# Per-strip DRAM tensors for a GNN layer's rows and partial sums, loaded from ScalarE's queue

## The chip, the cores and the metric

The kernel runs on one core of a Trainium2 chip. A core has five engines that run their own instruction streams: TensorE (PE, matrix products and transposes), VectorE (DVE), ScalarE (ACT), GpSimd (POOL) and SyncE (SP, which here only starts DMA transfers). ACT and POOL can start transfers too. An engine takes its instructions in the order of its stream and waits on semaphores; a transfer raises a semaphore when it has landed.

The metric is the device time of one execution in microseconds (us), the median over several runs. Lower is better.

## The reference: two graph layers on 3327 rows

Rows `x` (3327 x 128, padded to 3328) and a sparse symmetric adjacency `adj` (about 2% of the entries are not zero) go through two layers with a residual each. Layer 0 is a GATv2 attention with four heads, layer 1 a graph convolution:

```
h = relu(layernorm(x));  x = x + gatv2(h, adj, w1, w2, a, Wlin, w)      # layer 0
h = relu(layernorm(x))                                                   # layer 1
A_t = adj + I;  D_inv = rowsum(A_t) ** -0.5
x = x + relu(D_inv[:, None] * (A_t @ (D_inv[:, None] * (h @ W.T + b))))
```

Layer 1 is a dense product of the adjacency with 128-wide rows, so it can only be finished for a block of rows when layer 0 is finished for every block.

## The kernel before: blocks, strips and what each queue issues

**Blocks.** The 3328 rows are 26 blocks of 128 (`NB = 26`). Layer 0 runs block by block: POOL gathers the neighbours' rows (L595), PE transposes them (L622), VectorE makes the scores' input (L638), PE forms scores (L657) and sums (L670, L690). The generator `close` ends a block: ACT normalises (L754), PE and ACT apply two products (L771, L774, L782), VectorE writes the block's new rows `xn` (L786), SP stores them in DRAM (L788), ACT centres them (L793, L794), PE transposes (L798) and multiplies by layer 1's weights (L806), VectorE adds the bias (L809) and ACT puts the result into `x_sb` (L811). From then on the block is a column of layer 1's product.

**Strips.** Layer 1 is computed for strips of four blocks (`NS = 7`; strip 6 has two). A strip is one sum in PSUM, 128 x 512, over 26 columns, each column one matrix product of `x_sb[:, j]` with a 128 x 512 piece of the transposed adjacency (L1006). The pieces wait in DRAM (`AT_d`) and are brought in by L916, 11 columns at a time, alternately from SP and POOL. Much of the sum is made before the end, while layer 0 still runs: `part1` (columns known when the strip's own blocks are prepared, L379 to L387) and, for strips 1 to 3, `part2` (twelve more columns, L922 to L948). Both are stored in DRAM, `part1_d` and `part2_d`, and so are the new rows, `xn_d`. The last phase, `layer1`, multiplies the columns that are left: 26 for strip 0, then 12, 8, 4, 12, 8 and 4.

**The last phase in detail.** Strips 0 and 1 (`front`) are multiplied while block 25 is being closed; the column of block 25 itself comes last for both. `strip_in(s)` starts the loads of the strip's rows (L961), its `part1` (L963) and its `part2` (L965), each 256 KB; it is called at the fifth column of a strip, or at the last one where there are fewer or where the strip is in front. `strip_out(s)` ends a strip, three columns after its last one: VectorE adds `part2` (L973) and `part1` (L975), PE transposes the sum (L982), VectorE adds the block's own row and scales (L983, L984), takes the relu and adds the residual (L985), and ACT stores the result (L986). Strip 0 has no partial sums; ACT copies its sum (L977).

**Order.** The instructions of this phase stand in the order in which the Python code emits them (`tc.manual_schedule`); the framework adds the semaphore waits. SP issues, in this order: the pieces L916, strip 0's rows, more pieces, strip 1's three loads, block 25's store L788, the last three pieces, and then the loads of strips 2 to 6. ACT's stream in this phase is block 25's activations and the seven stores L986. Every transfer of SP and of ACT is given one of eight semaphores in turn (called lanes below), and its issue waits until the transfer before it on the same lane has landed. Buffers: `r0` (rows, and the sum in its second half) has three, `r1` (`part1`) two.

Of the kernel before, what the change touches and what calls it, by code (L numbers as in the profile page):

```python
# [9 lines left out]
F32 = mybir.dt.float32  # L10
# [5 lines left out]
P = 128  # L16
# [3 lines left out]
BANK = 512  # L20
# [211 lines left out]
def _sparse_layers(tc, nc, x, adj, w1, w2, a, wlin, w, gw, gb, gb_sb, gwT, x_sb, dinv, flag, ident, out):  # L232
# [13 lines left out]
    NP, D = x.shape  # L246
# [10 lines left out]
    with ExitStack() as l0:  # L257
        res = l0.enter_context(tc.tile_pool(name="res", bufs=1))
        dram = l0.enter_context(tc.tile_pool(name="dram", bufs=1, space=bass.MemoryType.DRAM))
        tables = [dram.tile([(NP + 1) * ROW], F32, name=f"table{k}") for k in range(2)]  # L260
        hT_d = dram.tile([P, NP], F32, name="hT_d")
        xn_d = dram.tile([NP, D], F32, name="xn_d")
        part1_d = dram.tile([D, NP], F32, name="part1_d")
        part2_d = dram.tile([D, NP], F32, name="part2_d")
        NS = -(-NB // 4)
        TURN = NP * P + HALF
        AT_d = dram.tile([NB * TURN], F32, name="AT_d")
        w1_sb = res.tile([P, H, D], F32, name="w1_sb")
# [59 lines left out]
        def bank():  # L328
            return ps_tr.tile([P, 4, P], F32, name="tr").rearrange("p a b -> p (a b)")
# [23 lines left out]
        def prep(b, k):  # L353
# [21 lines left out]
            def known_step(j0, js, at):  # L375
                assert all(blks[j0 + q].closed for q in js)
                pq = bank()
                for q in js:
                    nc.tensor.matmul(pq[:, :P], x_sb[:, j0 + q, :], at[:, q, :], start=(q == 0), stop=(q == js[-1]))  # L379
                yield  # L380
                if j0 == 0:
                    k.part1 = pb.tile([P, P], F32, name="part1", bufs=1)
                    nc.scalar.copy(k.part1, pq[:, :P])
                else:
                    nc.vector.tensor_add(k.part1, k.part1, pq[:, :P])
                if j0 + len(js) == finished(b):
                    nc.sync.dma_start(part1_d[:, b * P:(b + 1) * P], k.part1)  # L387

            known = []

# [353 lines left out]
        def close(k, hb):  # L744
            ag, b = k.ag, k.b
            yield

            rec = pv.tile([P, 2], F32, name="rec")
            nc.vector.reciprocal(rec, ag[:, :, WORK - 1])
            yield  # L750
            yield
            agn = pv.tile([P, 2, D], F32, name="agn")
            for u in range(2):
                nc.scalar.activation(agn[:, u, :], ag[:, u, :D], AF.Copy, scale=rec[:, u:u + 1])  # L754
            yield
            yield
            yield
            pt = ps_tr.tile([P, 4, P], F32, name="tr")
            for u in range(2):
                nc.tensor.transpose(pt[:, u, :], agn[:, u, :], ident)  # L760
            if hb == 0:
                k.agT = pv.tile([P, 16, H, 8], F32, name="agT")
            nc.scalar.copy(k.agT[:, 8 * hb:8 * hb + 8].rearrange("p t h q -> p (t h q)"), pt[:, :2].rearrange("p a b -> p (a b)"))
            yield
            if hb == 0:
                return

            yield
            po = ps_tr.tile([P, 4, P], F32, name="tr")
            for h in range(H):  # L770
                nc.tensor.matmul(po[:, h, :].rearrange("p (t q) -> p t q", q=8), wlinT[:, h, :], k.agT[:, :, h, :],  # L771
                                 start=True, stop=True)
            outT = pv.tile([P, H, P], F32, name="outT")
            nc.scalar.copy(outT, po)  # L774
            yield
            nc.vector.scalar_tensor_tensor(outT, outT, SLOPE, outT, op0=OP.mult, op1=OP.max)
            yield
            yield
            yield
            py = ps_tr.tile([P, 4, P], F32, name="tr")  # L780
            for h in range(H):
                nc.tensor.matmul(py[:, 0, :], outT[:, h, :], w_sb[:, h, :], start=(h == 0), stop=(h == H - 1))  # L782
            yield
            xn = pv.tile([P, D], F32, name="xn")
            st = pb.tile([P, 1], F32, name="st")
            nc.vector.scalar_tensor_tensor(xn, x_sb[:, b, :], 1.0, py[:, 0, :], op0=OP.mult, op1=OP.add, accum_out=st)  # L786
            nc.vector.tensor_scalar(st, st, -1.0 / D, None, op0=OP.mult)
            nc.sync.dma_start(xn_d[b * P:(b + 1) * P, :], xn)  # L788
            yield

            two = pv.tile([P, 2, D], F32, name="agn")
            cen, sq = two[:, 0], two[:, 1]
            nc.scalar.activation(cen, xn, AF.Relu, bias=st, scale=1.0)  # L793
            nc.scalar.activation(sq, xn, AF.Square, bias=st, scale=1.0, accum_out=k.dv[:, :1])  # L794
            yield
            yield
            pt = ps_tr.tile([P, 4, P], F32, name="tr")
            nc.tensor.transpose(pt[:, 0, :], cen, ident)  # L798
            nc.scalar.copy(sq, pt[:, 0, :])
            nc.vector.tensor_scalar(k.dv[:, :1], k.dv[:, :1], 1.0 / D, EPS, op0=OP.mult, op1=OP.add)  # L800
            yield
            rs = pb.tile([P, 2], F32, name="rs")
            yield from inv_root(rs, k.dv[:, :2])
            nc.vector.tensor_mul(dinv[:, b:b + 1], rs[:, 1:], k.dv[:, 2:])
            ph1 = ps_tr.tile([P, 4, P], F32, name="tr")
            nc.tensor.matmul(ph1[:, 0, :], sq, gwT, start=True, stop=True)  # L806
            yield
            yield
            nc.vector.scalar_tensor_tensor(cen, ph1[:, 0, :], rs[:, :1], gb_sb, op0=OP.mult, op1=OP.add)  # L809
            yield  # L810
            nc.scalar.activation(x_sb[:, b, :], cen, AF.Copy, scale=dinv[:, b:b + 1])  # L811
            k.closed = True
            yield
# [3 lines left out]
        for b in range(NB):  # L817
            k = Blk()
# [101 lines left out]
        def begin():  # L920

            work = [(s, j) for s in early for j in early[s]]  # L922
            pairs = [work[i:i + PAIR] for i in range(0, len(work), PAIR)]
            if not work:
                return
            thirds = pa.tile([P, NP], F32, name="adjb")[:, :3 * PAIR * BANK].rearrange("p (k j i) -> p k j i", k=3, j=PAIR)

            def bring(k):
                if k < len(pairs):
                    for to, of in columns(thirds[:, k % 3], pairs[k]):  # L930
                        nc.sync.dma_start(to, of)

            for k in range(3):
                bring(k)
            for _ in range(14):
                yield
            po = None
            for i, (s, j) in enumerate(work):
                assert blks[j].closed
                if j == early[s][0]:  # L940
                    po = bank()
                nc.tensor.matmul(po, x_sb[:, j, :], thirds[:, i // PAIR % 3, i % PAIR], start=(j == early[s][0]), stop=(j == early[s][-1]))  # L942
                if i % PAIR == PAIR - 1:
                    bring(i // PAIR + 3)
                if j == early[s][-1]:
                    part2 = pv.tile([P, H, P], F32, name="outT").rearrange("p h i -> p (h i)")
                    nc.scalar.copy(part2, po)
                    nc.sync.dma_start(part2_d[:, 4 * s * P:4 * s * P + BANK], part2)  # L948
                for _ in range(4):
                    yield  # L950

# [3 lines left out]
        def strip_in(s):  # L955

            n = min(4, NB - 4 * s)
            r0 = pr.tile([P, 2, BANK], F32, name="r0", bufs=3).rearrange("p k (b d) -> p k b d", b=4)[:, :, :n]
            r1 = pr.tile([P, 2, BANK], F32, name="r1").rearrange("p k (b d) -> p k b d", b=4)[:, :, :n]
            rows = slice(4 * s * P, (4 * s + n) * P)  # L960
            nc.sync.dma_start(r0[:, 0], xn_d[rows, :].rearrange("(b p) d -> p b d", p=P))  # L961
            if finished(4 * s):
                nc.sync.dma_start(r1[:, 0], part1_d[:, rows].rearrange("p (b i) -> p b i", b=n))  # L963
            if s in early:
                nc.sync.dma_start(r0[:, 1], part2_d[:, rows].rearrange("p (b i) -> p b i", b=n))  # L965
            return n, rows, r0, r1

        def strip_out(s, po, n, rows, r0, r1):
# [19 lines left out]

        front = range(min(2, NS - 1))
        work = [(s, j) for s in front for j in range(first_column(s), NB - 1)]  # L990
        in_front = len(work)
        work += [(s, NB - 1) for s in front] + [(s, j) for s in range(len(front), NS) for j in range(first_column(s), NB)]
        pieces = [work[i:i + PIECE] for i in range(0, len(work), PIECE)]
# [216 lines left out]
        with tc.manual_schedule():  # L1210
# [4 lines left out]
            n = len(groups)  # L1215
# [8 lines left out]
            for i in range(-1, n + 1):  # L1224
                if i + 1 < n:
                    slot()
                if 0 <= i < n:
                    b, hb, m = groups[i]
# [153 lines left out]
```

## Time and profile before

| | us |
|---|---|
| median of 8 runs | 2482.07 (2480.44 to 2486.53) |
| the profiled execution: its own time | 2482.38 |
| the profiled execution: span of its instructions | 2480.2 |
| PE busy | 2226.2 (90%) |
| VectorE busy | 2053.5 (83%) |
| ACT busy | 639.6 (26%) |
| POOL busy | 1767.9 (71%) |
| DMA engines, mean share busy | over 0.9 in nearly all of the span |

The span runs from the first to the last instruction; the execution's own time has 2.2 us more around it. A slice of the page is 62 us, and the last phase of layer 1 is about one slice and a half: PE is busy to 6 tenths in the last of them, VectorE to 3. In the views below a line such as `PE tr L982 <- DVE r L975: 14.2, 3, 11.8` reads: instructions of PE of line 982 that write tile `tr` sat idle until VectorE's line 975 had written `r`, 14.2 us in all, 3 times, 11.8 us the longest.

### The profile page before, as it was taken

The page shows a single profiled execution, that of the slowest core. Times are in us where ns is not written, and L with a number is a line of the kernel's source. Part 1 is how long each engine was busy: PE and PEld are TensorE (multiplying, and loading weights), DVE is VectorE, ACT ScalarE, POOL GpSimd, SP SyncE. Part 2 cuts the span into 40 slices and gives each one's busy share as a digit, 9 for nine tenths or more (in the row PEclk, how much of TensorE's full clock was granted, in tenths as well). Part 3 has the DMA queues.
Part 4 walks back from the last instruction along what each step waited for, and adds up shares of the span by engine and source line. Part 5 has one row for each costly group of instructions (what it writes and reads, how often), then busy time and mean ns, then how long its engine had stood idle before and what let it go on. Part 6 is the DMA issues. An engine that isn't in the chain of part 4 may idle for free.

```text
span 2480.2 us, 51942 instructions
## 1 busy us (share of the span) xinstructions
PE 2226.2 (90%) x19254; PEld 1595.2 (64%) x19254; DVE 2053.5 (83%) x6426; ACT 639.6 (26%) x1547; POOL 1767.9 (71%) x1867
## 2 busy tenths in 40 slices
PE   6589889989988998998999999899999999999996
PEld 4466666666666666666676676666667667666653
DVE  7688988898898888889889888988888988896633
ACT  4122222223222222322222222232222222221110
POOL 3577777777777777777777777777777777777760
PEclk9699999999999999999999999999999999999998
DMA  9999999999999999999999999999999999999996
GB/s 301 381 351 320 352 327 326 350 358 323 332 367 326 321 353 338 322 343 359 325 331 359 340 323 345 347 315 332 356 329 321 356 342 316 340 334 332 364 305 175
DMA packets 401715, 826.93 MB, mean 333 GB/s; under 512 B 38435, under 2 KB 270383, under 8 KB 398127
## 3 DMA queue, kind: packets, MB, share of 16 engines
q0 software_dynamic: 144464, 628.85, 71.8%
q1 hardware_dynamic: 165343, 147.87, 18.9%
q10 hardware_dynamic: 91648, 46.80, 6.3%
q8 instruction: 155, 2.54, 0.4%
q14 instruction: 105, 0.86, 0.1%
HBM read 754.47 MB, written 113.22 MB: 350 GB/s over the span
## 4 chain that ended last, share of the span: by engine, by line
PE 40%; DVE 24%; DMA 17%; POOL 11%; issue 6%; SPq 2%; ACT 1%; DVEq 0%; ACTq 0%; POOLq 0%
PE z L622 14%; DVE r L638 13%; DMA g<-table,idx 13%; POOL g L595 11%; PE s L657 10%; DVE cand L422 3%; PE ag L670 2%; PE z L627 2%; PE tr L379 1%; DVE cand L456 1%; DVE lists L453 1%; SPq L916 1%; PE tr L942 1%; PE z L1124 1%; DVE codes L410 1%
## 5 line engine op out<-in xcount | busy, mean ns | idle before, releaser
L595 POOL DMA_INDIRECT g<-table,idx x1664 | 1614.1, 970 | 577.4 <-issue 414.0
L638 DVE TENSOR_TENSOR r<-z,x1n 128x1024 f32<-128x1024 f32 x832 | 1011.3, 1216 | 131.8 <-PE z L622 129.6
L622 PE MATMUL z<-ident,g 128*128 128x128 f32 x6656 | 924.2, 278 | 105.3 <-DVE r L638 97.7
L622 PEld LDWEIGHTS z<-ident,g 128*128 128x128 f32 x6656 | 753.3, 142 | 241.5 <-DVE r L638 146.1
L657 PE MATMUL s<-r,sel 128*4 128x512 f32 (+1 forms) x3744 | 507.5, 581 | 10.4 <-DVE r L638 10.1
L657 PEld LDWEIGHTS s<-r,sel 128*4 128x4 f32 x3744 | 86.3, 85 | 256.9 <-issue 180.9
L698 ACT COPY ssb<-s 128x512 f32<-128x512 f32 x208 | 121.9, 586 | 498.6 <-PE s L657 498.1
L422 DVE MAX8 cand<-codes 128x8 f32<-128x52 uint16 x1664 | 218.2, 208 | 0.0
L670 PEld LDWEIGHTS ag<-g,wt 128*32 128x32 f32 x3328 | 117.2, 110 | 102.5 <-issue 95.3
L670 PE MATMUL ag<-g,wt 128*32 128x133 f32 x3328 | 159.1, 278 | 0.0
L633 DVE TENSOR_TENSOR r<-z,x1n 128x128 f32<-128x128 f32 x104 | 30.0, 289 | 152.2 <-PE z L627 149.8
L730 ACT ACTIVATE sc<-sc 128x32 f32<-128x32 f32 x208 | 47.9, 230 | 414.4 <-DVE sc L725 255.3
L367 ACT COPY at<-tr 128x512 f32<-128x512 f32 (+1 forms) x175 | 97.1, 555 | 213.4 <-PE tr L365 201.0
L453 DVE MAX8 lists<-cand 128x8 f32<-128x272 f32 (+1 forms) x338 | 133.4, 395 | 2.2
L365 PE MATMUL tr<-ident,adjb 128*128 128x128 f32 x676 | 107.9, 282 | 26.2 <-DMA adjb<-in_adj_dram 16.4
L635 ACT ACTIVATE r<-z 128x512 f32<-128x512 f32 x104 | 62.1, 597 | 258.8 <-DVE r L633 258.8
L709 PE MATMUL tr<-ident,ssb 128*128 128x128 f32 x832 | 124.9, 273 | 1.7 <-ACT ssb L698 1.7
L627 PE MATMUL z<-oi,x1b 128*128 128x256 f32 x416 | 125.2, 383 | 0.0
L595 POOL DMA_INDIRECT ge<-table,idxo x104 | 98.4, 946 | 32.2 <-issue 13.3
L456 DVE MATCH_REPLACE8 cand<-lists,cand 128x272 f32<-128x272 f32 (+1 forms) x312 | 118.1, 378 | 0.0
L410 DVE SCALAR_TENSOR_TENSOR codes<-adjb,code 128x832 uint16<-128x832 f32 x104 | 104.2, 1018 | 12.5 <-DMA adjb<-in_adj_dram 12.5
L622 PE MATMUL z<-ident,ge 128*128 128x128 f32 x416 | 83.1, 282 | 26.5 <-DVE r L638 26.4
(200 smaller groups left out, 2444.1 us busy)
## 6 DMA issues: line engine op xcount, KB each, us to landing
adjb<-in_adj_dram SPq DMA_DIRECT2D x26, 1664.0 KB
table<-AT_d SPq DMA_DIRECT2D x26, 1664.0 KB
AT_d<-at ACTq DMA_DIRECT2D x150, 256.0 KB
g<-table,idx POOLq DMA_INDIRECT x1664
table<-img SPq DMA_DIRECT2D x12, 1296.0 KB
adjb<-AT_d SPq DMA_DIRECT2D x72, 128.0 KB
g<-AT_d SPq DMA_DIRECT2D x25, 256.0 KB
g<-AT_d POOLq DMA_DIRECT2D x25, 256.0 KB
```

What stands on the lines that cost most here:

```text
L410: nc.vector.scalar_tensor_tensor(codes[:, i], adjb[:, c0:c0 + part], 0.0, code[:, c0:c0 + part], op0=OP.not_equal, op1=OP.mult, accum_out= ...
L422: nc.vector.max(cand[:, c, 8:].rearrange("p (r s) -> p r s", s=32)[:, :, sgm % 32], codes.rearrange("p a b -> p (a b)")[:, sgm % 32 * SEG: ...
L453: nc.vector.max(top, of)
L456: nc.vector.match_replace(out=of, in_to_replace=top, in_values=of, imm_value=0.0)
L595: return nc.gpsimd.indirect_dma_start(out=g[:, t, lo:hi], out_offset=None, in_=tab, in_offset=bass.IndirectOffsetOnAxis(ap=at[:, t:t + 1], ...
L622: nc.tensor.matmul(z[:, i, q * P:(q + 1) * P], g[:, m % 2 * 4 + q, c0:c0 + D], ident, is_transpose=True, start=(q == 0 or m < 8), stop=(m ...
L627: nc.tensor.matmul(z[:, i, :n], k.x1b[:, h * D:(h + 1) * D], k.oi[:, hb * n:(hb + 1) * n], start=False, stop=True, skip_group_check=True)
L638: nc.vector.tensor_tensor(r.rearrange("p h (i s) -> p h i s", s=16), z.rearrange("p h (i s) -> p h i s", s=16), k.x1n[:, 2 * hp:2 * hp + 2 ...
L657: nc.tensor.matmul(k.s[32 * h:32 * h + 4, :n], sel[:, h, 31 - row:35 - row], r[h // 2][:, h % 2, :n], start=(row == 0), stop=(last and (m ...
L670: nc.tensor.matmul(k.ag[32 * cg:32 * cg + 32, u, :WORK], wt[:, t].rearrange("p h q -> p (h q)"), g[:, t, f0:f0 + WORK], start=(w == 0 and ...
L698: nc.scalar.copy(ssb, s)
L709: nc.tensor.transpose(pt[:, q, :], ssb[:, q * P:(q + 1) * P], ident)
```

## The change

New rows, `part1` and `part2` get one DRAM tensor for each strip, 128 x 512, in place of one for all rows; a block's store writes a 128-column slice of its strip's tensor. The rows lie transposed in blocks, so that each of 128 partitions reads 2 KB in one piece in L961, where it read four pieces of 512 B. The three loads of `strip_in` are started by ACT in place of SP. Nothing else differs; line numbers after the first edit fall by two.

```diff
-        xn_d = dram.tile([NP, D], F32, name="xn_d")
-        part1_d = dram.tile([D, NP], F32, name="part1_d")
-        part2_d = dram.tile([D, NP], F32, name="part2_d")
         NS = -(-NB // 4)
+        xn_d, part1_d, part2_d = ([dram.tile([P, 4 * P], F32, name=f"{name}{s}") for s in range(NS)] for name in ("xn_d", "part1_d", "part2_d"))
...
-                    nc.sync.dma_start(part1_d[:, b * P:(b + 1) * P], k.part1)
+                    nc.sync.dma_start(part1_d[b // 4][:, b % 4 * P:(b % 4 + 1) * P], k.part1)
...
-            nc.sync.dma_start(xn_d[b * P:(b + 1) * P, :], xn)
+            nc.sync.dma_start(xn_d[b // 4][:, b % 4 * P:(b % 4 + 1) * P], xn)
...
-                    nc.sync.dma_start(part2_d[:, 4 * s * P:4 * s * P + BANK], part2)
+                    nc.sync.dma_start(part2_d[s], part2)
...
-            nc.sync.dma_start(r0[:, 0], xn_d[rows, :].rearrange("(b p) d -> p b d", p=P))
+            nc.scalar.dma_start(r0[:, 0], xn_d[s][:, :n * P].rearrange("p (b d) -> p b d", b=n))
             if finished(4 * s):
-                nc.sync.dma_start(r1[:, 0], part1_d[:, rows].rearrange("p (b i) -> p b i", b=n))
+                nc.scalar.dma_start(r1[:, 0], part1_d[s][:, :n * P].rearrange("p (b i) -> p b i", b=n))
             if s in early:
-                nc.sync.dma_start(r0[:, 1], part2_d[:, rows].rearrange("p (b i) -> p b i", b=n))
+                nc.scalar.dma_start(r0[:, 1], part2_d[s][:, :n * P].rearrange("p (b i) -> p b i", b=n))
```

## The prediction

> **What bounds the kernel now.** Nothing before layer 1's last phase is touched except where a few stores land, so I read that phase. First the busy times of seven stretches of it.
>
> ```profile
> core 0: us, PE busy (x) PEld busy (x) DVE busy (x) ACT busy (x) POOL busy (x), PEclk, DMA share, GB/s
> 2395.00:2417.00 22.00, 22.00 (x89) 11.41 (x88) 2.80 (x15) 2.37 (x7) 15.26 (x23) 1.00 1.11 290
> 2417.00:2428.00 11.00, 10.77 (x30) 4.55 (x28) 1.14 (x7) 1.25 (x3) 3.48 (x5) 1.00 1.09 292
> 2428.00:2440.00 12.00, 0.37 (x2) 0.37 (x3) 1.81 (x3) 0.00 (x0) 0.00 (x0) 0.67 1.05 292
> 2440.00:2451.00 11.00, 11.00 (x30) 5.37 (x29) 6.91 (x11) 0.00 (x0) 0.00 (x0) 0.89 0.67 198
> ```
>
> PE works without a gap until 2428 and again from 2440, and stands still for 12 us between; the DMA engines are full (about 290 GB/s, 0.9 us for 256 KB) until 2440. What PE waits for is in the chain of waits (start, length, what).
>
> ```profile
> 2431.70 0.77 SPq L961
> 2432.47 0.35 issue
> 2432.82 0.41 SPq L963
> 2433.22 0.05 issue
> 2433.28 4.79 DMA r<-part_d
> ...
> 2438.16 0.70 DVE r L973
> ...
> 2438.89 0.70 DVE r L975
> ...
> 2439.63 1.12 PE tr L982 x4
> ```
>
> Strip 1's partial sums are issued by SP only at 2433.28, behind the pieces of L916, and land at 2438.07. PE's own timeline says what that costs and what stands on both sides:
>
> ```profile
> 2417.04 0.27 PE L798 MATMUL tr<-ident,agn 128*128 128x128 f32 x1
> 2417.15 4.46 PE L1006 MATMUL z<-g,x_sb 128*128 128x512 f32 x10
> ...
> 2426.39 0.60 PE L982 MATMUL tr<-ident,r 128*128 128x128 f32 x4
> 2426.82 1.02 PE L1006 MATMUL z<-g,x_sb 128*128 128x512 f32 x2
> 2439.63 1.12 PE L982 MATMUL tr<-ident,r 128*128 128x128 f32 x4 [11.79 <-DVE r L975]
> ```
>
> After 2439.63 PE is nearly always busy: strips 2 to 6 have their L982 at 2448.31, 2452.63, 2463.42, 2469.45 and 2472.62, with idle times of 0.28 and 2.13 us alone. The last view is who waits on SP:
>
> ```profile
> SPq L916 <- DMA r<-xn_d: 1.1, 1, 1.1
> ```
>
> A piece of the adjacency, which has no data in common with strip 0's rows, was held until those rows had landed (2403.87; it was issued at 2403.89). That is the lane: a queue's issue waits for the transfer eight places before it, whoever started that, and stands still meanwhile.
>
> **The change part by part (lines numbered as before).** *Removed from SP:* 16 issues. Ahead of the last pieces they took 1.44 us (strip 0, 2397.61 to 2399.05) and 2.1 us (strip 1, 2431.70 to 2433.82). The DMA engines are full there, so this moves landings by at most 1.44 us; the last pieces land at 2440.8 and are used at about 2465, so 24 us cover them.
>
> *Layout:* a store still writes 128 pieces of 512 B and a load reads 2 KB pieces. Stores of `xn` land 4 to 5 us after their issue (217.27 to 221.44, 2433.82 to 2438.31) and are read strips later; priced at nothing, and at 1 us if only the last one, strip 6's, were waited for. If a load gains, it is inside the landing bounds below.
>
> *Strip 0's load on ACT* stands behind the copy L698 (ends 2387.28) and ahead of L730. In the order of the built kernel its lane belongs to a piece issued at 2385.18 that lands at 2390.85. So ACT goes on at 2390.85 + 0.42 (an L986 issue) = 2391.3, and L730 moves from 2388.78 by 2.5 us. VectorE's L664 to L681 then end at 2394.2 in place of 2391.7; PE needs them at 2396.66 (L670) and 2399.08 (L690). Covered; 2.5 us if it were not.
>
> *Strip 1's three loads on ACT* are the core. They stand between L774 (ends 2410.06) and L793, block 25's centring (2414.39). Their lanes belong to the pieces that before were issued at 2410.36, 2416.04 and 2424.49 and landed at 2425.48, 2430.00 and 2431.33. ACT can't reach L793 until the third has landed. Behind L793 stand L794, L799, L811 and every later ACT instruction; L798 on PE waits for it, and PE's stream stands. When is ACT free? Upper bound: landing as before, 2431.33 + 0.42 = 2431.75. Lower: issue 1.44 us earlier and the shortest issue-to-landing nearby (2429.63 to 2434.27, 4.64): 2423.05 + 4.64 + 0.42 = 2428.1. In between: POOL's last three transfers (landed 2427.3 to 2429.6) now wait for PE's columns behind L798, so three times 0.9 us of DMA work leave, one or two loads of strip 1 enter, and the SP gain comes on top: about 2.3 us early, 2429.45. I take that.
>
> PE's L798 follows L793's start by 0.40 + 0.14 (weights): 2430.0 in place of 2417.04, a stall of 13. From there to strip 1's L982 lie 10.80 us of work (2417.04 to 2427.84). After the present stall PE was slow at first: 1.12 for 0.60, and 7.94 for eight columns that take 6.86 (0.43 each half), 1.6 us; that now falls here. Strip 1's L982: 2442.4 in place of 2439.63, **+2.8** (+1.4 to +5.0). Strip 1's data are there by then, so the old wait is gone and a longer one has come.
>
> The Trainium skill, "TensorE: Matmul & The Clock Gate", part 1, has the clock fall to half after an idle window of some 3.4 us and rise after as much work; the row shows a granted 0.67 and 0.89. By the rule 3.4 us at half clock cost about 1.7, by the rows 1.6.
>
> *Strips 2 to 6 on ACT.* Each strip's loads now stand behind the store L986 of the strip before, which waits for L985. From a strip's L982 to the end of L985: 0.67 + 2.14 = 2.81 (2448.31, 2448.95, 2451.09). L986 starts 0.04 later; each issue takes 0.5 with its gap (2445.65, 2446.11, 2446.62). So the last of three loads starts at 4.35, of two at 3.85. Landing: between 3.06 (L961 of strip 5) and 4.65 (L961 of strip 4, with others in flight) for 256 KB; 3.9 with three loads and a store, 3.4 with two; strip 6's 128 KB 2.6 (2.25 alone; 3.06 at most). Then 0.09, one or two additions of 0.70 (0.42 in strip 6), 0.06. L982 to L982:
>
> strip 1 to 2: here L985 of strip 1 ends 3.52 after its L982, since strip 0's three operations come first; 5.06 + 3.9 + 1.57 = 10.5, before 8.68. Strip 2 to 3: 4.35 + 3.9 + 1.57 = 9.8, before 4.32. Strip 3 to 4: PE's twelve columns are longer than the loads, 10.79 as before, plus 0.6 for a slow start (0 to 1.6): 11.4. Strip 4 to 5: 3.85 + 3.4 + 0.85 = 8.1, before 6.03. Strip 5 to 6: 3.85 + 2.6 + 0.57 = 7.0, before 3.17. Sum 46.8 against 32.99: **+13.8** (+10.9 with the shortest landings, +17 with the longest). Before, a strip's rows and `part2` were issued while the strip before was still being ended, and `part1` waited only for the strip two before it.
>
> Another rule speaks against the change. "DMA: Bandwidth & Descriptors", anatomy of one DMA, says that a DMA's semaphore wait is made on the issuing sequencer before dispatch. By it ACT stands still through each lane wait, as summed here; without it the 2.8 would be an 11.8 gain. The trace shows such waits on SP; no row has an ACT computation held behind one.
>
> **The sum:** 2482.38 + 2.8 + 13.8 = 2499.0, against the profiled execution, which is 0.3 above the median shown: **2498.7**. Its own range: 2482.4 + 1.4 + 10.9 = 2494.7 to 2482.4 + 5.0 + 17 = 2504.4.
>
> **The rivals.**
>
> *Faster: ACT's loads run ahead.* If a waiting transfer on ACT doesn't hold the activations and stores behind it, strip 1's L982 comes at 2427.84, and strips 2 to 6 keep their old spacing without the slow start: 11.8 + 1.6 = 13.4 less, **2469**. For it: the gap is real, and all pieces that PE needs next have landed by 2436. Against it: the order of the streams, and SP, which did stand still for a lane. It decides if L793 starts near 2414.
>
> *No change: the front stall goes, the strips serialise.* If ACT is free before PE reaches L798, strip 1 is at 2427.84 and strip 6 at 2427.84 + 46.8 - 0.6 = 2474.0, 1.4 later than now: **2483.5**. For it: the lane waits are inferred from an order, not seen on ACT. Against it: the third lane's piece was issued at 2424.49, so it can't land by 2417.
>
> *Worse: the loads land later.* Store and loads of a strip share ACT's queue, the DMA may serve 1 MB in a row, and PE may be slow after each stall of 3 to 6 us (1 us each): 5 to 8 more, **2506**. Against it: the DMA share is 0.47 and 0.13 in the last stretches.
>
> **How the numbers follow.** Forecast 0.78; faster 0.06; no change 0.08; worse 0.08. About 0.2% (5 us) is what a measurement of this kernel can tell. The range runs from 2491 (ACT free 1 us before its lower bound, +0.4, and every load landing in 2.25 us, +8.5) to 2505, into the worse case. Faster 0.06, within 0.2% 0.08, slower 0.86.
>
> **What would show it.** ACT: strip 1's three loads with gaps before each, L793 at 2429 to 2432 right behind the third. PE: a gap of 11 to 15 us ahead of L798, none ahead of strip 1's L982; then gaps ahead of L982 in strips 2, 3, 5 and 6, released by VectorE's additions, which wait for `r<-part`. Each strip's loads directly behind the store of the strip before. I am wrong if PE passes L798 at 2417, or if strips 2 and 3 lie less than 9 us apart.

## The result, and the profile after

The change makes the kernel slower: a median of 2498.33 us (2495.24 to 2507.4, 13 runs) against 2481.93 us of the kernel before on the same chip (2475.74 to 2488.85, 35 runs). The ratio is 1.0071, with a 95% interval of 1.0062 to 1.0081, so 15.4 to 20.1 us (it compares all runs of the two kernels; the quotient of the medians alone is 1.0066). The profiled execution took 2494.81 us, with a span of 2492.7: 12.5 us more than before's 2480.2.

First the busy times of four stretches of the phase (the columns are those of the view before: PE, PEld, DVE, ACT, POOL, then the granted clock, the DMA share and GB/s).

```profile
2417.00:2428.00 11.00, 0.33 (x2) 0.33 (x3) 0.00 (x0) 0.78 (x3) 0.00 (x0) 0.66 1.06 292
2428.00:2440.00 12.00, 11.92 (x30) 5.18 (x30) 4.70 (x19) 1.27 (x4) 2.24 (x3) 0.88 0.82 236
2440.00:2451.00 11.00, 7.99 (x26) 3.84 (x25) 4.75 (x7) 0.00 (x0) 0.00 (x0) 1.00 0.39 120
2451.00:2462.00 11.00, 7.24 (x17) 3.06 (x16) 4.80 (x7) 0.00 (x0) 0.00 (x0) 0.84 0.30 97
```

The stretch without PE has moved forward by one row: it was 2428 to 2440 and is now 2417 to 2428. Behind 2440, where PE used to be busy all the time, it now works some 70% of it, with a DMA share of 0.39 and 0.30: PE waits there, and not for a full memory system. ACT's timeline shows the first wait (start, length, instruction, and in brackets the idle time before it and its releaser).

```profile
2408.10 0.59 ACT L772 COPY outT<-tr 128x512 f32<-128x512 f32 x1 [2.24 <-PE tr L769]
2423.75 0.34 ACTq L959 DMA_DIRECT2D r<-xn_d  x1
2425.47 0.33 ACTq L961 DMA_DIRECT2D r<-part_d  x1
2426.76 0.35 ACTq L963 DMA_DIRECT2D r<-part_d  x1
2427.22 0.40 ACT L791 ACTIVATE agn<-xn,st 128x128 f32<-128x128 f32 x1 [18.53 <-DMA r<-xn_d]
```

Strip 1's three loads are issued at 2423.75, 2425.47 and 2426.76, each within 0.03 us of the landing of a piece (2423.73, 2425.45, 2426.74). Block 25's centring, L791, comes only behind the third, 18.53 us after ACT's last work. Its bracket names the rows' load, but in all six profiles with these loads on ACT L791 starts 0.45 or 0.46 us after the issue of the third load starts, whenever the rows land; so it is that issue which holds it. PE's timeline carries that on, and shows the later waits:

```profile
2427.68 0.47 PE L796 MATMUL tr<-ident,agn 128*128 128x128 f32 x1 [11.85 <-ACT agn L791]
2427.94 5.91 PE L1004 MATMUL z<-g,x_sb 128*128 128x512 f32 x10
...
2439.94 0.60 PE L980 MATMUL tr<-ident,r 128*128 128x128 f32 x4
...
2450.42 0.63 PE L980 MATMUL tr<-ident,r 128*128 128x128 f32 x4 [3.01 <-DVE r L973]
...
2459.93 0.66 PE L980 MATMUL tr<-ident,r 128*128 128x128 f32 x4 [3.76 <-DVE r L973]
...
2478.38 0.66 PE L980 MATMUL tr<-ident,r 128*128 128x128 f32 x4 [1.46 <-DVE r L973]
...
2485.02 0.69 PE L980 MATMUL tr<-ident,r 128*128 128x128 f32 x2 [5.55 <-DVE r L973]
```

Strip 1's transposes (L980, L982 before) come at 2439.94 with no wait, against 2439.63: the old wait of 11.79 us is gone, and one of 11.85 stands 12 us ahead of it. From there on four of five strips wait. The chain of waits tells for what, here for strip 2:

```profile
2442.78 0.70 DVE r L983
2443.51 0.40 ACTq L984
...
2443.94 0.52 ACTq L959
...
2444.78 0.35 ACTq L961
...
2445.16 3.60 DMA r<-part_d
...
2449.58 0.70 DVE r L973
...
2450.42 0.64 PE tr L980 x4
```

Strip 1's last VectorE operation (L983) releases its store on ACT (L984); behind the store, on the same queue, stand strip 2's loads (L959, L961, then L963 at 2445.16); the last lands 3.60 us later, VectorE adds, PE goes on. Strips 3, 5 and 6 repeat it, with 3.60, 2.92 and 2.20 us for the landing.

### The profile page after: what moved, and what is told of

It is laid out like the page before. It is cut to its first block, busy times and chain, and to the rows that moved or that the text cites. A ratio compares the mean times of both kernels' runs of the same rounds, so it can differ in the third digit from the quotient of the medians.

```text
span 2492.7 us, 51935 instructions
## 1 busy us (share of the span) xinstructions
PE 2225.1 (89%) x19254; PEld 1593.4 (64%) x19254; DVE 2052.7 (82%) x6426; ACT 641.6 (26%) x1547; POOL 1771.3 (71%) x1867
## 4 chain that ended last, share of the span: by engine, by line
PE 40%; DVE 28%; DMA 16%; POOL 9%; issue 5%; SPq 1%; ACT 1%; ACTq 0%; DVEq 0%; POOLq 0%
DVE r L636 15%; PE z L620 14%; DMA g<-table,idx 12%; PE s L655 10%; POOL g L593 9%; DVE cand L420 4%; PE ag L668 2%; PE z L625 2%; PE tr L377 2%; DVE codes L408 2%; DVE cand L454 1%; DVE lists L451 1%; PE tr L940 1%; DMA adjb<-in_adj_dram 1%; PE tr L363 1%
## 5 line engine op out<-in xcount | busy, mean ns | idle before, releaser
L668 PEld LDWEIGHTS ag<-g,wt 128*32 128x32 f32 x3328 | 116.8, 110 | 102.9 <-issue 96.0
L668 PE MATMUL ag<-g,wt 128*32 128x133 f32 x3328 | 158.9, 278 | 0.0
L728 ACT ACTIVATE sc<-sc 128x32 f32<-128x32 f32 x208 | 48.3, 232 | 417.2 <-DVE sc L723 254.3
L377 PE MATMUL tr<-at,x_sb 128*128 128x128 f32 x488 | 71.9, 287 | 38.7 <-DVE sc L723 31.6
```

Of the source, the lines that this page charges most:

```text
L668: nc.tensor.matmul(k.ag[32 * cg:32 * cg + 32, u, :WORK], wt[:, t].rearrange("p h q -> p (h q)"), g[:, t, f0:f0 + WORK], start=(w == 0 and ...
```

## Experiments

Times of one row were taken on one chip beside the kernel before. "Front wait" is PE's wait for block 25's centring or ahead of strip 1's transposes, whichever there is; "strips" is the time from strip 1's to strip 6's transposes. Both are from the profiled execution.

| kernel | median us | ratio to before, 95% interval | front wait us | strips us |
|---|---|---|---|---|
| before | 2482 to 2484 | | 11.79 | 32.99 |
| the change | 2498.33 | 1.0071 (1.0062 to 1.0081) | 11.85 | 45.08 |
| layout alone | 2483.75 | 1.0003 (0.9989 to 1.0017) | 11.13 | 34.10 |
| queue alone | 2503.29 | 1.0085 (1.0065 to 1.0106) | 11.93 | 49.19 |
| strips 2 to 6 on ACT | 2497.22 | 1.0067 (1.0046 to 1.0089) | 9.59 | 48.34 |
| strips 0, 1 on ACT | 2484.29 | 1.0007 (0.9993 to 1.0022) | 12.49 | 32.30 |
| stores on SP | 2484.68 | 1.0008 (0.9999 to 1.0018) | 11.90 | 32.42 |
| all loads on POOL | 2481.34 | 0.9995 (0.9985 to 1.0006) | 1.22 | 41.74 |
| strip 1 early on SP | 2480.10 | 0.9994 (0.9985 to 1.0004) | none | 43.18 |
| strips 0, 1 on POOL | 2480.60 | 0.9995 (0.9982 to 1.0008) | 0.64 | 41.69 |
| all early | 2476.34 | 0.9977 (0.9963 to 0.9991) | none | 37.10 |
| all early, no prefetch | 2491.45 | 1.0038 (1.0024 to 1.0052) | none | 49.42 |

### Layout or queue?

Two kernels make one half of the change each. The layout alone, with the three loads of `strip_in` back on SP:

```diff
-            nc.scalar.dma_start(r0[:, 0], xn_d[s][:, :n * P].rearrange("p (b d) -> p b d", b=n))
+            nc.sync.dma_start(r0[:, 0], xn_d[s][:, :n * P].rearrange("p (b d) -> p b d", b=n))
```

> The layout alone: a DRAM tensor per strip, the loads back on SP as before. Theory (the layout is priced at nothing, everything comes from the queue): the time of before, 2480 to 2484, ratio 0.999 to 1.001; the stall ahead of strip 1's transposes stays at 11 to 12.5 us and the spacing of the transposes of strips 1 to 6 sums to 32 to 34 us. Rival (the layout carries part of the cost, since a whole tensor's last store now gates a load): 4 us or more slower, 2486 and up.

The queue alone, the kernel before with its three loads on ACT:

```diff
-            nc.sync.dma_start(r0[:, 0], xn_d[rows, :].rearrange("(b p) d -> p b d", p=P))
+            nc.scalar.dma_start(r0[:, 0], xn_d[rows, :].rearrange("(b p) d -> p b d", p=P))
```

> The queue alone: the loads on ACT, the three DRAM tensors as before. Theory: the time of the changed kernel, 2495 to 2500; PE's first transpose behind block 25's centring waits 11 to 13 us, strips 1 to 6 sum to 44 to 47 us. Rival (layout carries part): more than 4 us below the changed kernel, 2494 or less.

The layout alone is the kernel before (1.0003; strips in 34.10 us, where 32 to 34 were expected). The queue alone is the whole cost: 1.0085, and its interval meets that of the change. It came out above what was expected, 2503.29 in place of at most 2500, and its strips took 49.19 us, not 44 to 47, in a profile of its slowest run (2509.78). PE's timeline from strip 3's transposes on shows most of that:

```profile
2471.69 1.11 PE L982 MATMUL tr<-ident,r 128*128 128x128 f32 x4 [5.88 <-DVE r L975]
2472.59 12.91 PE L1006 MATMUL z<-g,x_sb 128*128 128x512 f32 x24
```

Of the 4.1 us above the change, 2.9 lie between strips 3 and 4, where PE was slow; the last pair of runs looks at that. The other 1.3 us are spread over the other strips, and their cause was not tested.

### The front or the strips behind it?

The same switch by strip, in the changed kernel, once each way round:

```diff
+            eng = nc.scalar if s > 1 else nc.sync
-            nc.scalar.dma_start(r0[:, 0], xn_d[s][:, :n * P].rearrange("p (b d) -> p b d", b=n))
+            eng.dma_start(r0[:, 0], xn_d[s][:, :n * P].rearrange("p (b d) -> p b d", b=n))
```

> The loads of strips 0 and 1 on SP as before, those of strips 2 to 6 on ACT. Theory: the front is as before (PE passes the transpose behind block 25's centring near 2417, then waits 11 to 12.5 us ahead of strip 1's transposes), and strips 1 to 6 sum to 44 to 47 us in place of 33: +11 to +14, so 2493 to 2496. Rival (the held activations of the front are what costs): the time of before, 2480 to 2485.

> The loads of strips 0 and 1 on ACT, those of strips 2 to 6 on SP as before. Theory: PE waits 11 to 13 us for block 25's centring and not at all ahead of strip 1's transposes, which come 1 to 4 us later than before; strips 1 to 6 sum to 32 to 35 us: 2483 to 2486. Rival (the front is what costs): 2494 or more.

Strips 2 to 6 on ACT carry the cost (1.0067), and a little more of it than expected: 2497.22 for 2493 to 2496, with strips of 48.34 us for 44 to 47 and a front wait of 9.59 for 11 to 12.5. The front on ACT costs 1.7 us by the ratio, with an interval that holds no change, although the wait it makes is there in full (lines of this kernel are one higher behind L959):

```profile
2430.00 0.48 PE L796 MATMUL tr<-ident,agn 128*128 128x128 f32 x1 [12.49 <-ACT agn L791]
...
2443.33 0.60 PE L981 MATMUL tr<-ident,r 128*128 128x128 f32 x4
```

PE stands 12.49 us ahead of L796 and then passes strip 1's transposes without a stop. One wait has taken the place of the other at nearly the same length.

### Is it the store in front of the loads, or ACT's queue itself?

The changed kernel with one word different: the output stores go by SP, the loads stay on ACT.

```diff
-            nc.scalar.dma_start(out[rows, :].rearrange("(b p) d -> p b d", p=P), xo)
+            nc.sync.dma_start(out[rows, :].rearrange("(b p) d -> p b d", p=P), xo)
```

> The changed kernel with the strips' output stores on SP in place of ACT, so that no load stands behind a store. Theory (strips 2 to 6 lose their time because each load waits behind the store of the strip before): the wait of 11 to 13 us for block 25's centring stays, the spacing of the transposes of strips 1 to 6 falls from 45 to 32 to 36 us: 2483 to 2488. Rival (loads issued by ACT land late by themselves, or ACT is slow to issue them): the spacing stays at 42 to 47 us and the time at 2494 or more.

All of the expected numbers were met: a front wait of 11.90, strips in 32.42, 2484.68 us. PE's timeline has strip 1's transposes and strip 6's this far apart:

```profile
2438.91 0.60 PE L980 MATMUL tr<-ident,r 128*128 128x128 f32 x4
...
2471.33 0.57 PE L980 MATMUL tr<-ident,r 128*128 128x128 f32 x2 [2.13 <-DVE r L973]
```

ACT's timeline has strip 2's loads where the store no longer holds them:

```profile
2435.15 0.59 ACT L975 COPY r<-z 128x512 f32<-128x512 f32 x1 [1.21 <-PE z L1004]
2435.16 0.33 ACTq L959 DMA_DIRECT2D r<-xn_d  x1
2440.42 0.39 ACTq L961 DMA_DIRECT2D r<-part_d  x1
```

Strip 2's rows start at 2435.16, right at strip 0's copy, and its `part1` at 2440.42, when strip 0's last addition frees the buffer, not at 2443.94 and 2444.78 behind strip 1's store. So loads started by ACT are as good as loads started by SP; loads behind a store that waits for the strip before are not.

### What is the front wait worth?

Three kernels take the front wait away, or nearly. All loads on POOL (`eng = nc.gpsimd` in `strip_in` of the changed kernel):

> The changed kernel with all loads of the strips on POOL. POOL's transfers don't take turns with those of SP and ACT, POOL issues no store, and no activation stands behind it. Theory (the place of the issue, not the transfers, costs the time): PE passes the transpose of block 25's centring near 2417 and strip 1's transposes near 2428 without a wait over 2 us; strips 1 to 6 sum to 31 to 35 us: 9 to 14 us faster than before, 2468 to 2474. Rival (the gap of 12 us is a full memory system that nothing gets past): a wait of 8 us or more at strip 1 or strip 2, and 2478 to 2485.

The kernel before with strip 1's loads ahead of the pieces on SP:

```diff
-                if j == min(NB - 1, first_column(s) + 4 * (s not in front)):
+                if i == 0:
+                    ins.update((f, strip_in(f)) for f in front)
+                elif s not in front and j == min(NB - 1, first_column(s) + 4):
```

> The kernel before with one thing changed: strip 1's three loads are issued by SP at once with strip 0's, ahead of the pieces, not behind them. Theory: strip 1's transposes come near 2428 with no wait over 2 us; strip 2's loads still stand behind SP's pieces (2436 before), so strip 2 waits until 2440 to 2444, and the time falls by 4 to 9 us: 2473 to 2479. Rival (the pieces that SP issues later are waited for instead): 2480 to 2486.

And strips 0 and 1 on POOL, the others on SP (`eng = nc.sync if s > 1 else nc.gpsimd`):

> The loads of strips 0 and 1 on POOL, those of strips 2 to 6 on SP. Theory: no wait over 2 us ahead of strip 1's transposes, strip 2 waits for its loads, which stand behind SP's pieces, until 2440 to 2444: 2473 to 2479, and so 3 to 7 us above the kernel with all loads on POOL. Rival (strip 2's loads are not late): the same time as that kernel, within 2 us.

The wait ahead of strip 1 fell to 1.22 us or less in all three, as the theory had it, and nearly none of the time went with it: 0.9994 and 0.9995, with intervals that hold no change. The expected gains of 4 to 14 us did not come; the times lie in the ranges of the rivals. PE's timeline of the kernel with strip 1 early on SP has the reason:

```profile
2427.98 0.60 PE L982 MATMUL tr<-ident,r 128*128 128x128 f32 x4
2428.41 7.03 PE L1008 MATMUL z<-g,x_sb 128*128 128x512 f32 x16
2445.61 1.08 PE L982 MATMUL tr<-ident,r 128*128 128x128 f32 x4 [10.17 <-DVE r L975]
```

The chain of waits ahead of that last line has:

```profile
2438.27 5.69 DMA r<-part_d
```

Strip 1 is 11.65 us earlier than before, and strip 2 only 2.7 us (2445.61 for 2448.31): its loads still stand on SP behind the last pieces (issued up to 2438.27) and the last needs 5.69 us to land while the DMA engines are busy (share 1.08). With strips 0 and 1 on POOL strip 2 waited 7.67 us in the same way. With all loads on POOL the wait was spread over strips 1 to 3 (1.22, 2.95 and 3.82 us), and no wait reached the 8 us of a memory system that nothing gets past; yet the two kernels with loads on POOL came out 0.7 us apart, not the 3 to 7 expected. The chain of that kernel shows what strip 3's waited for:

```profile
2431.11 6.57 DMA g<-AT_d
...
2437.70 0.02 ACTq L985
...
2437.76 5.54 DMA out_dram<-r
...
2443.85 0.49 POOL r L960
```

Strip 0's store on ACT was held until a piece landed at 2437.68 (a lane again), took 5.54 us, and only then was the buffer free into which strip 3's rows are loaded.

### Can the wait be taken away altogether?

The next kernel (from the kernel before) frees the loads from pieces, lanes and buffers at once; the other edit of the pair leaves out the prefetch of strips 3 to 6.

```diff
-            r1 = pr.tile([P, 2, BANK], F32, name="r1").rearrange("p k (b d) -> p k b d", b=4)[:, :, :n]
+            r1 = pr.tile([P, 2, BANK], F32, name="r1").rearrange("p k (b d) -> p k b d", b=4)[:, :, :n] if finished(4 * s) else None
+            eng = nc.gpsimd if s > 2 else nc.sync
...
-            ot, t, xo = r0[:, 1], r1[:, 1], r0[:, 0]
+            ot, t, xo = r0[:, 1], r0[:, 1], r0[:, 0]
...
-            nc.scalar.dma_start(out[rows, :].rearrange("(b p) d -> p b d", p=P), xo)
+            (nc.scalar if s == NS - 1 else nc.gpsimd).dma_start(out[rows, :].rearrange("(b p) d -> p b d", p=P), xo)
...
-                if j == min(NB - 1, first_column(s) + 4 * (s not in front)):
-                    assert len(ending) < 2
-                    ins[s] = strip_in(s)
+                if i == 0:
+                    ins.update((f, strip_in(f)) for f in range(3))
+                elif 2 <= s < NS - 1 and j == min(NB - 1, first_column(s) + 4):
+                    ins[s + 1] = strip_in(s + 1)
```

> The kernel before with the loads freed from everything that held them in the runs so far: strips 0, 1 and 2 are loaded by SP at once, ahead of the pieces; strips 3 to 6 are loaded by POOL, each while the strip before it is being summed; the output stores of strips 0 to 5 go by POOL; and the sums with x reuse the second half of a strip's rows, so that a strip's other buffer is free once its partial sum has been added. Theory (the stall of 12 us only moved to strips 2 and 3 because their loads stood behind pieces, lanes and buffers): no wait over 3 us ahead of the transposes of strips 1 to 5, the last transposes near 2462 in place of 2472.6: 2470 to 2475. Rival (the transfers themselves are the bound until 2440, so PE waits for the late pieces or loads wherever they stand): a wait of 5 us or more at strip 2 or 3 or in their columns, 2477 to 2483.

> The same kernel, but strips 3 to 6 are loaded by POOL in the fourth column of their own strip, behind the store of the strip before, as the changed kernel does on ACT. Theory (a load behind the store of the strip before costs 3 to 6 us a strip wherever the columns between are short): strips 2 to 3, 4 to 5 and 5 to 6 grow to 9 to 10, 7 to 8 and 6 to 7 us, so 9 to 13 us above the kernel that loads a strip early. Rival (only ACT's queue does that): within 3 us of it.

With everything early the time is 0.9977 of before (0.9963 to 0.9991): 2 to 9 us faster, and the fastest kernel of this study. Its 2476.34 us lie between the 2470 to 2475 of the theory and the 2477 to 2483 of the rival. The last transposes came at 2466.02, between what the theory (2462) and the kernel before (2472.62) had, since one wait of 4.08 us was left, ahead of strip 3:

```profile
2436.58 6.21 DMA r<-part_d
...
2443.59 0.70 DVE r L976
...
2444.34 1.06 PE tr L983 x4
2445.40 11.59 PE z L1008 x24
```

Its last load, issued at 2436.58, took 6.21 us, while the DMA engines were still full (share 1.09 in 2428 to 2440, at 303 GB/s). Here the rival was partly right: up to 2440 the transfers do set a limit.

Without the prefetch, strips 2 to 3, 4 to 5 and 5 to 6 took 10.64, 9.41 and 8.42 us in place of 8.11, 6.03 and 3.17, each above its expected range (9 to 10, 7 to 8, 6 to 7), and the whole 15.1 us more than with it, where 9 to 13 were expected. In the profiles the strips make 12.3 of the difference (49.42 less 37.10). Another 4.0 lie ahead of strip 1, whose transposes came at 2432.92 and not at 2428.92: PE waited there 2.91 and 0.39 us for pieces, and with the prefetch 1.32. The two programs are the same up to there, so this part is not shown to belong to the prefetch. These loads stand behind stores on POOL's queue, not ACT's: the cost belongs to the order of store and load, whichever engine issues both.

### Where do the last microseconds between profile and median come from?

The profiled execution of the change was 12.5 us longer than before's, the medians differ by 16.4. The changed kernel was profiled twice more.

> The changed kernel once more, for a second profile of it. Its profiled execution gained 12.5 us on before's, its median 16 to 18. Theory (TensorE runs slowly for a while after a wait of 5 us or more, and where that falls on strip 3's 24 columns they set the time): an execution of 2498 us or more has strip 3's transposes at 1.1 us in place of 0.66 and its 24 columns at 12 to 13 us in place of 10.47, one of 2496 or less has not. Rival (the scatter comes from before this phase): the 24 columns take 10.4 to 10.6 us whatever the time, and the transposes of block 25 come later by the difference.

> The changed kernel a third time; both theories expect of it what they expect of the second profile.

The second took 2493.12 us, the third 2500.67. PE's timeline at strips 2 and 3, of the second and then of the third:

```profile
2449.03 0.63 PE L980 MATMUL tr<-ident,r 128*128 128x128 f32 x4 [3.16 <-DVE r L973]
2449.50 5.29 PE L1004 MATMUL z<-g,x_sb 128*128 128x512 f32 x8
2458.40 0.66 PE L980 MATMUL tr<-ident,r 128*128 128x128 f32 x4 [3.61 <-DVE r L973]
2458.89 10.47 PE L1004 MATMUL z<-g,x_sb 128*128 128x512 f32 x24
```

```profile
2455.07 0.63 PE L980 MATMUL tr<-ident,r 128*128 128x128 f32 x4 [3.37 <-DVE r L973]
2455.53 3.60 PE L1004 MATMUL z<-g,x_sb 128*128 128x512 f32 x8
2464.30 1.12 PE L980 MATMUL tr<-ident,r 128*128 128x128 f32 x4 [5.18 <-DVE r L973]
2465.21 11.52 PE L1004 MATMUL z<-g,x_sb 128*128 128x512 f32 x24
```

In the second, PE was slow in strip 2's eight columns (5.29 us for 3.60), whose time is hidden in the wait that follows. In the third these ran at full speed, so the wait behind them was longer (5.18 for 3.61), and PE was slow where it counts: 1.12 us for the transposes and 11.52 for the 24 columns, 1.5 us from strip 3 to 4. The granted clock agrees: 0.72 in 2449 to 2455 of the second, 1.00 in 2455 to 2459.2 and 0.59 in 2464.3 to 2468 of the third. With the first ten columns (7.35 us for 5.68) slow running makes some 3.1 us of the 7.5 between the two spans. The rest, 4.5 us, was there before this phase: L780 is at 2414.55 in the third and at 2410.09 in the second. So both theories hold a part, and the 12 to 13 us expected of the columns were too many. The queue alone (24 columns in 12.91 us) and strips 2 to 6 on ACT (12.24) show the same slow stretch, and without its 2.9 and 2.2 us their strips would lie in the range expected (46.3 and 46.2).

## Why the prediction was right

Predicted: 2498.7 us; measured: 2498.33. The mechanism was the one forecast, and its parts can be set beside the trace. Two terms were 1 and 2 us too large, and PE's slow stretches after the waits between strips were priced at 0.6 us in all, so the closeness of the total is partly luck.

**What is priced at nothing** was nothing as far as the runs show: the layout (1.0003), and of SP's issues that were taken away, which no run tests alone, only that PE waits for no piece in this phase of the profile. Strip 0's load held L728 until 2389.78. The profiled execution of after was 1.37 us ahead at this time (2395.29 at L668 for 2396.66 at L670 before), so this is 2.4 us late on the clock of before; 2.5 were forecast, and PE's L668 passed in its turn as the cover said.

**Strip 1's loads on ACT** were held by lanes, as derived. The profiled execution was still 1.37 us ahead by L780 (2411.34 for L782's 2412.71), so 2427.22 for the centring is 2428.6 on the clock of before: inside the bounds of 2428.1 and 2431.75, 0.85 below the value taken. The stall was 11.85 (13 forecast), and from L796 to strip 1's transposes it took 12.26 us (10.80 plus 1.6 forecast). So strip 1 came 1.7 us late where +2.8 was forecast: 0.31 by the trace, plus the 1.37. The run with strips 0 and 1 alone on ACT gives 1.7 by its ratio, with an interval from -1.7 to 5.5.

**Strips 2 to 6.** The forecast of 10.5, 9.8, 11.4, 8.1 and 7.0 was measured as 10.48, 9.51, 10.80, 7.65 and 6.64: 12.1 us more than before in place of 13.8. The terms that were too large are the landings: 3.60 after the last of three issues (3.9), 2.92 of two (3.4), 2.20 for strip 6 (2.6); and the 0.6 for a slow start behind strip 3's wait, which was 0 in this execution and 1.5 to 2.9 in others; the 0 to 1.6 given for it was too narrow, and the +17 of the upper bound left it at 0.6.

**The sum** for the profiled execution is therefore -1.37 + 1.68 + 12.09 + 0.1 (behind strip 6's transposes) = 12.5, 4 us under the forecast, while the medians differ by 16.4. Of those 3.9 us, 1.37 is the early phase of the one execution; most of the others can be PE's slow stretches after waits, which fall at different places from run to run (from strip 3 to 4, against 10.80, 1.5 us more in the third profile and 2.2 and 2.9 in the runs of 48 and 49 us). How the 13 runs share them was not measured. The forecast had these stretches mostly in the rival "worse"; they are a part of the ordinary case.

**The rivals.** That ACT's loads run ahead is refuted by L791, which starts right behind the third load, not near 2414. Its price was doubtful as well: it counted the whole wait ahead of strip 1 as a gain of 11.8 us. The three kernels without that wait, or with 1.2 us of it, were 0.6 to 1.9 us faster by their medians, with intervals that hold no change, because strip 2's loads, behind pieces, a lane or a buffer, were late next. The front half of the change, a wait of 12 us on ACT, cost so little for the reason forecast: the old wait of nearly that length went. "No change" fell with the third lane, as argued. "Worse" was right about slow PE and wrong about the landings, which were shorter than assumed.

The two rules of the Trainium skill that the prediction weighed: "DMA: Bandwidth & Descriptors", anatomy of one DMA, has the wait for a semaphore on the issuing sequencer (in a section on transfers from GpSimd); L791's 18.53 us behind loads that ACT issued agree. "TensorE: Matmul & The Clock Gate", part 1, has the clock fall after some 3.4 us of idleness. Every wait of PE over 5 us in this phase was followed by slow instructions, as that says (granted clock 0.50 in 2471 to 2477 of the queue alone, 0.58 in 2456 to 2462 of strips 2 to 6 on ACT). Of ten waits of 2.95 to 4.08 us ahead of strips 2, 3 and 5, six were and four were not, among the slow ones 2.95 and 3.01, among the others 3.76: near 3.4 us the length of the wait alone doesn't tell.

## What to carry to other kernels

A queue works in order, as ACT's and POOL's did here, so a load takes over every wait of what stands in front of it: put next to a store that waits for the item before, it turns a pipeline into a series (12 us over five strips here, undone by moving the stores alone). Moving transfers to an idle engine is free only if nothing that others need stands behind them there and if its issues don't wait; ask for each issue which data, buffer and lane it waits for. And before a wait is priced as a gain, look for what is late next: 12 us without PE all but vanished from their place in three kernels, and the time stayed, until loads, buffers and stores were freed together, which gained 2 to 9 us.

## What the runs showed of the hardware

TensorE's slow stretch does not always begin where a wait ends: behind a wait of 3.16 us the transposes of strip 2 took 0.63 us as usual, and the eight columns after them 5.29 for 3.60 (granted clock 0.72); in another execution the slow part fell behind the next wait. The same kernel can so lose 1.5 us or nothing at strip 3, with no difference in its instructions.

While the DMA engines were full, a transfer was late from either of two queues: 256 KB landed 6.21 us after POOL's issue (2436.58, all early) and 5.69 us after SP's (2438.27, strip 1 early), against 3.60 and 2.92 us after ACT's later on, where the DMA share was 0.3 to 0.4.
